# A two-layer cross-attention kernel: its beginning written out in order on every engine, with text keys by k tile and the first slot's stacks ahead of the second entry's queries

## The chip, the cores and the metric

One core of a Trainium2 chip runs the kernel. The metric is the device time of one execution in microseconds; the time before is the median of three runs. The engines are TensorE (PE, with its weight loads as PEld), VectorE (DVE), ScalarE (ACT), GpSimd (POOL) and SyncE (SP), whose queue issues nearly all transfers.

## The reference

Two cross-attention layers in turn, each on 16 entries of 256 tokens x 320 channels with a context of 256 x 512 per entry, 20 heads of 16. The first 77 context rows are text in layer 0, the others image tokens (in layer 1 all but the last four are text). Cut to what matters, layer 0 is:

```python
q = x @ Wq; k_text = text @ Wk; v_text = text @ Wv
ip_k = ip @ Wk_ip; ip_v = ip @ Wv_ip
text_out = softmax(q_h k_h^T * scale) v_h
text_probs = softmax(q k_text^T * scale)          # all heads together
sem = (text_probs @ text) @ ip^T * scale
ip_out = (softmax(q_h ip_k_h^T * scale + 0.5 * sem) * spatial_mask) ip_v_h
x = (text_out + ip_out) @ Wout + bout + x
```

Layer 1 is alike, with the semantic term by head and normalised. All is float32; the kernel splits operands into a rounded part and a rest ("halves", `hi` and `lo`) and adds three products for one.

## The kernel before

The work of a layer is cut into 80 slots: 16 entries times 5 groups of 4 heads. For a slot k of layer 0 the tiles `ks` and `qs` (a ring of four pairs, the "stack") hold up to 127 rows: keys or queries in three parts (48 rows, loaded back from DRAM, `kd` and `qd`, where they were written in another layout), 77 rows of the semantic term (`M` in `ks`, the text probabilities `tph` in `qs`), and two rows for the maxima (fields `ind0` through `mt` in `ks`, the maxima through `mt` in `qs`). `stacks0(k, parts)` issues these loads: K, Q, T (`tph`) and M. `score0` makes the scores (PE, bank S) and their maxima (DVE), `maxima0` turns the maxima and sends them into `qs`, `turned0` makes the turned scores (bank T), whose exponentials go on to `attend0` (values).

Ahead of the slots of an entry stand its tasks, generators that are advanced a step at a time: `k0` (keys, for a pair of entries), `q0` (queries), `m0t` (`tokens0`, the gram of text and image rows, tile `M`), `s0` (`semantic0`: products, softmax, transposes, `tph`, and the factor `rs`) and `v0` (three value parts). For the first pair, `keys_first` makes the keys; the text keys are made one column block m after the other, each over all four k tiles of 128 context channels.

What sets the order: everything behind `begin()` is scheduled with PE alone pinned to the written order, other engines follow the scheduler's own estimate. `begin()` (L1165) is pinned on all engines. But the loads and splits of the first weights, contexts and x (`all_halves`, L220, called at L286 to L304), the constants (zeroing of `ks`, `qs`, `vr`; L309 to L335) and the load of the fields (`ind0`, L311) stand ahead of `begin()`, outside the pinned part, so the scheduler places them among its instructions. All loads go through one helper (`dma`, L83) on SP's queue. A load of the second and third dozen waits for the landing of the one eight places earlier, since eight semaphores serve them in turn.

PSUM banks: three X, two T, one P, and S. Before, every product of the tasks goes to X.

Of the kernel before, what the change touches and what calls it, by code (L numbers as in the profile page):

```python
# [49 lines left out]
def xattn2(  # L50
# [38 lines left out]

    def bank(tag="X"):  # L90
        return ps.tile([128, 512], F32, tag=tag, name=tag, bufs=BANKS[tag])
# [35 lines left out]
    nc.scalar.copy(ident_r, ident)  # L127
    tmask = const_tile([128, 7], "tmask")
    dma(tmask, tmask_d)
# [90 lines left out]
    def all_halves(jobs, rings):  # L220

        waiting = []
        for src, hi, lo, tag in jobs:
            while sum(w[3] == tag for w in waiting) == rings[tag]:
                halves(*waiting.pop(0)[:3])
            raw = buf(tag, [128, 512], bufs=rings[tag])
            raw = raw[:, : src.shape[1]] if len(src.shape) == 2 else raw.rearrange("p (k n) -> p k n", k=src.shape[1])
            dma(raw, src)
            waiting.append((hi, lo, raw, tag))
        for w in waiting:  # L230
            halves(*w[:3])

# [29 lines left out]
    def context(b, n, wait=0):  # L262
# [9 lines left out]
        if n == 2:  # L272
# [3 lines left out]

    ct = [buf(t, [128, 2, 512], FR, bufs=2, name="ct") for t in ("cta", "cta", "ctb", "ctb")]
    ctx0 = [(cT_d[k * 128 : (k + 1) * 128, : 2 * S], ct[k][:, 0], ct[k][:, 1]) for k in range(4)]
# [6 lines left out]
    RINGS = {"P": SIZES["NP"], "raw": SIZES["RAW"], "rawc": 2}  # L285
    all_halves(  # L286
        [job for k in range(4) for job in (
            (*ctx0[k], ("rawc", "raw")[k // 2]), (rows(wk0_d, k), *rounded(wkt[:, k]), "P"))],
        RINGS,
    )  # L290
    x0 = buf("xq", [128, 3, S])
    dma(x0, xT_d[0].rearrange("(k p) t -> p k t", p=128))
    all_halves(
        [(rows(wq0_d, k), *rounded(wqt[:, k]), ("rawc", "raw")[k // 2]) for k in range(3)]
        + [(rows(wki0_d, k), *rounded(w), "P") for k, w in enumerate(wkit)],
        RINGS,
    )
    nc.vector.tensor_scalar_mul(wqt[:, 2, CH : 2 * CH], f(wqt[:, 2, CH : 2 * CH]), tmask[:, 3:4])
    wvt, wvit = buf("wC", [128, 2, 4, 320], FR), [buf("wD", [128, 2, 2, 320], FR, bufs=2) for j in range(2)]
    all_halves(  # L300
        [(rows(wv0_d, k), wvt[:, 0, k], wvt[:, 1, k], ("rawc", "raw")[k % 2]) for k in range(4)]
        + [(rows(wvi0_d, k), wvit[k // 2][:, 0, k % 2], wvit[k // 2][:, 1, k % 2], ("rawc", "raw")[k % 2]) for k in range(4)],
        RINGS,
    )  # L304
    wv0, wvi0 = [lambda s, k: wvt[:, s, k]], [lambda s, k: wvit[k // 2][:, s, k % 2]]
    wq, wo = [lambda s, k, m: wqt[:, k, columns(s, m)]], []

# [3 lines left out]
    ind0 = buf("raw", [128, 512], bufs=SIZES["RAW"], name="ind0")[:2, :S]  # L311
    dma(ind0, ind0_d)
    ind0r = buf("mt", [8, S], FR, name="ind0r")[:2]
    nc.scalar.copy(ind0r, ind0)
    for i in range(SIZES["NR"]):
        nc.gpsimd.memset(f(ks[i]), 0.0)
        nc.gpsimd.memset(f(qs[i]), 0.0)
        dma(ks[i][XROW + T0 : KS0], ind0r.unsqueeze(1).to_broadcast([2, 4, S]))
# [3 lines left out]
    for v in vr:  # L322
        nc.gpsimd.memset(v, 0.0)
        for t in range(2):
            nc.vector.tensor_scalar_add(
                vcols(v, V0W)[:, t, :, 16], vcols(v, V0W)[:, t, :, 16], tmask[:, t : t + 1]
            )
        nc.vector.memset(vcols(v, V0W)[:, 2, :, 16], 1.0)
# [3 lines left out]
    nc.vector.memset(zone, 0.0)  # L332
    nc.vector.memset(zone[:, 21:22], 1.0)
    hsn = const_tile([128, 3, 8, 2, 16], "hsn")
    nc.gpsimd.memset(f(buf("q", [128, 2, 3, S], FR))[64:, :, 2], 0.0)  # L335
# [37 lines left out]
    def keys_first():  # L373
# [6 lines left out]
        for w, lo, hi, a, z in ((wk0, 0, T0 + 1, 0, T0), (wki0, T0 - 1, S, T0, S)):  # L380
            for m in range(3):
                kp = bank()[:, : 2 * (hi - lo)].rearrange("p (b t) -> p b t", b=2)
                prod_m(kp, w, m, lambda s, k: ct(s, k)[:, :, lo:hi], 4)
                n = 64 if m == 2 else 128
                evacuate(kst[m][:, 0, :, a:z], kst[m][:, 1, :, a:z], kp[:, :, a - lo : z - lo], m)
                if a:
                    keys_out(kd[0][0], m, kst[m], slice(0, 1))
                else:
                    nc.gpsimd.tensor_copy(kt[:n, m, :, :, :T0], f(kst[m][:n, :, :, :T0]))
                yield  # L390
# [188 lines left out]
    def split(src, neg, eng, tag):  # L579

        hl = buf(tag, [128, 5, S], FR)
        order = queued if tag == "hq" else lambda inst: inst
        order(nc.scalar.copy(hl[:, 0:3], src))  # L583
        order(eng.tensor_sub(hl[:, 3:5], src[:, 0:2], f(hl[:, 0:2])))  # L584
        order(nc.vector.scalar_tensor_tensor(hl[:, 2], f(hl[:, 2]), neg, src[:, 2], op0=ALU.mult, op1=ALU.add))  # L585
        return hl

# [42 lines left out]
    def queries0(b):  # L630
        x = x0 if b == 0 else load(xT_d[b], "xq")
        yield
        xs = split(x, tmask[:, 5:6], nc.gpsimd if b else nc.vector, "hq")
        yield
        return (yield from queries(0, xs))
# [529 lines left out]
    def begin():  # L1165
        parts = lambda *keys: [step(key) for key in keys if key in tasks]
        k0, q0, s0, m0, q1 = ("k0", 0), ("q0", 0), ("s0", 0), ("m0t", 0), ("q0", 1)
        parts(k0, k0, k0, q0, q0, q1, q0, q0, q0)
        get(*q0)
        get(*m0)  # L1170
        parts(s0, s0, s0, s0, s0)
        stacks0(0, "M")
        stacks0(1, "M")
# [121 lines left out]
```

## Time and profile before

| | us |
|---|---|
| median of three runs (1550.27 to 1552.6) | 1551.0 |
| the profiled execution | 1552.99 |
| its span, first to last instruction | 1551.2 |
| granted PE clock over the span | 0.971 |
| PE busy | 1450.1 |
| DVE busy | 1220.5 |
| POOL busy | 1193.5 |
| ACT busy | 872.6 |

A row of a timeline gives the start from the beginning of the span, the duration, the engine, the line of the kernel, the operation, `out<-in` with the tiles' names, the shape and how many equal instructions follow each other; in brackets the time that the engine was idle ahead of it and what ended that. SPq and ACTq are the engines' queues issuing transfers. A row of a stretch gives the busy time and count of PE, PEld, DVE, ACT and POOL, then PE's granted clock (1 is full), the DMA engines' busy share and GB/s.

### The profile page before, as it was taken

What the parts mean: (1) busy time and instruction counts of PE and PEld (TensorE: products, weight loads), DVE (VectorE), ACT (ScalarE), POOL (GpSimd) and SP (SyncE); (2) the same over time, 40 slices, a digit from 0 to 9 for tenths busy, and PEclk for the clock granted to TensorE, in tenths of its full rate; (3) what the DMA queues carried; (4) which work ended last, traced back from release to release, by engine and by line L of the source; (5) the groups of instructions that cost most, each with busy time, mean ns of one, the idle gap of its engine ahead of it and who ended that gap; (6) DMA issues with size and microseconds to landing.
All of it is one profiled execution on the core that took longest, in us unless ns stands there. A gap on an engine that the chain in (4) does not pass through costs nothing.

```text
span 1551.2 us, 36088 instructions
## 1 busy us (share of the span) xinstructions
PE 1450.1 (93%) x12726; PEld 1170.3 (75%) x12726; DVE 1220.5 (79%) x2687; ACT 872.6 (56%) x1941; POOL 1193.5 (77%) x1246
## 2 busy tenths in 40 slices
PE   6789999999999989878999999999999999999996
PEld 6668787888787878656777777777777777777764
DVE  6468877778887788878778887888888888788785
ACT  5335464556464545536566666666656665666561
POOL 4248797889797877768578798878887898779785
PEclk9889999999999999889999999999999999999998
DMA  6755767676767665666344344434444444433411
GB/s 210 196 180 153 220 189 213 181 219 189 218 191 214 180 206 165 189 181 178 102 137 124 109 123 129 124 110 142 110 114 124 126 116 118 137 106 99 118 32 36
DMA packets 228815, 233.04 MB, mean 150 GB/s; under 512 B 38410, under 2 KB 198508, under 8 KB 228620
## 3 DMA queue, kind: packets, MB, share of 16 engines
q1 hardware_dynamic: 226428, 229.44, 51.6%
q8 instruction: 102, 1.67, 0.5%
q10 hardware_dynamic: 2208, 1.30, 0.3%
q14 instruction: 77, 0.63, 0.1%
HBM read 118.04 MB, written 77.10 MB: 126 GB/s over the span
## 4 chain that ended last, share of the span: by engine, by line
PE 33%; POOL 7%; DVE 6%; ACT 2%; issue 2%; DMA 1%; ACTq 1%; SPq 0%; DVEq 0%; POOLq 0%
PE X L923 11%; PE X L238 5%; POOL wt L914 5%; PE P L935 3%; PE X L595 3%; PE P L945 3%; PE T L875 2%; PE S L881 2%; DVE wt L924 2%; PE X L1048 1%; POOL hq L584 1%; DVE ho L585 1%; DVE mn L883 1%; ACTq L905 1%; PE X L248 1%
## 5 line engine op out<-in xcount | busy, mean ns | idle before, releaser
L758 POOL TENSOR_TENSOR P<-P,rs 128x512 f32<-128x512 f32 x320 | 412.8, 1311 | 126.9 <-ACT P L755 126.7
L914 POOL TENSOR_TENSOR wt<-P,ctb 128x512 f32<-128x512 f32 x320 | 410.3, 1307 | 88.7 <-ACT ctb L913 87.8
L923 PE MATMUL X<-ctb,gm 128*128 128x512 f32 x1120 | 306.5, 403 | 6.4 <-DVE wt L924 6.3
L755 ACT ACTIVATE P<-T 128x512 f32<-128x512 f32 x320 | 176.1, 594 | 177.0 <-PE T L752 107.1
L924 DVE TENSOR_TENSOR wt<-X,wt 128x512 f32<-128x512 f32 x320 | 216.7, 682 | 47.0 <-PE X L923 40.8
L923 PEld LDWEIGHTS X<-ctb,gm 128*128 128x128 f32 x1120 | 196.2, 189 | 39.6 <-DVE wt L924 9.2
L895 ACT ACTIVATE P<-T 128x512 f32<-128x512 f32 x320 | 173.3, 594 | 79.3 <-PE T L875 76.0
L913 ACT ACTIVATE ctb<-P 128x512 fp32r<-128x512 f32 x320 | 187.4, 627 | 47.8 <-PE X L923 35.9
L883 DVE TENSOR_REDUCE mn<-S 128x4 fp32r<-128x1008 f32 x160 | 191.3, 1195 | 0.0
L730 DVE TENSOR_REDUCE mn<-S 128x4 fp32r<-128x716 f32 x160 | 142.3, 889 | 0.0
L785 PE MATMUL P<-P,vr 128*32 128x256 f32 x1920 | 129.9, 404 | 2.8 <-DVE mx L665 1.8
L728 PE MATMUL S<-ks,qs 125*128 125x256 f32 x640 | 119.5, 311 | 9.0 <-DMA qs<-tph 4.8
L728 PEld LDWEIGHTS S<-ks,qs 125*128 125x128 f32 x640 | 90.7, 199 | 45.0 <-issue 36.6
L752 PE MATMUL T<-qs,ks 127*128 127x256 f32 x640 | 110.4, 294 | 13.8 <-DVE tmp L802 7.7
L1011 POOL TENSOR_TENSOR r<-u,rs 128x40 f32<-128x40 f32 (+2 forms) x17 | 108.7, 6394 | 3.8 <-DVE u L1008 3.8
L752 PEld LDWEIGHTS T<-qs,ks 127*128 127x128 f32 x640 | 92.8, 198 | 17.1 <-DVE tmp L802 8.1
L729 DVE TENSOR_REDUCE mn<-S 128x4 fp32r<-128x308 f32 x160 | 74.2, 463 | 30.1 <-PE S L728 29.5
L796 DVE STREAM_TRANSPOSE nt<-P 128x512 f32<-128x512 f32 x80 | 56.9, 711 | 47.7 <-PE P L785 47.2
L785 PEld LDWEIGHTS P<-P,vr 128*32 128x32 f32 x1920 | 58.3, 115 | 45.8 <-issue 9.4
L595 PE MATMUL X<-hq,wE 128*128 128x256 f32 x512 | 80.4, 297 | 9.0 <-ACT hq L583 4.3
L935 PE MATMUL P<-P,v1t 128*32 128x256 f32 x1280 | 86.5, 388 | 0.2 <-DVE wt L924 0.2
L945 PE MATMUL P<-wt,zone 128*32 128x256 f32 x1280 | 85.1, 379 | 0.3 <-DVE wt L924 0.3
(231 smaller groups left out, 3011.9 us busy)
## 6 DMA issues: line engine op xcount, KB each, us to landing
qd<-q SPq DMA_DIRECT2D x96, 256.0 KB
qs<-tph SPq DMA_DIRECT2D x64, 308.0 KB
rawc<-in_cT_dram SPq DMA_DIRECT2D x60, 256.0 KB
qs<-qd SPq DMA_DIRECT2D x80, 192.0 KB
ks<-kd SPq DMA_DIRECT2D x80, 192.0 KB
ks<-kd SPq DMA_DIRECT2D x160, 96.0 KB
qs<-qd SPq DMA_DIRECT2D x160, 96.0 KB
kd<-kst SPq DMA_DIRECT2D x57, 256.0 KB
```

Of the source, the lines that this page charges most:

```text
L728: mm(sp[:, h], Q[: XROW + T0, h, t * 128 : (t + 1) * 128], K[: XROW + T0, h], start=True, stop=True)
L730: anchor(nc.vector.tensor_reduce(mn[:, t, :, 1], sp[:, :, T0:], axis=AX.X, op=ALU.max))
L752: mm(st[p][:, j], K[:KS0, 2 * p + j, t * 128 : (t + 1) * 128], Q[:KS0, 2 * p + j], start=True, stop=True)
L755: exp = anchor(nc.scalar.activation(pt, st[p], AF.Exp, scale=SCALE))
L758: anchor(nc.gpsimd.tensor_mul(pt, pt, rs[:, t : t + 1].to_broadcast([128, 2, S])))
L785: mm(pv[32 * s : 32 * s + 32, o : o + S], v[:, vt, h : h + 32], P[k, s // 2][:, t, s % 2], start=vt < 2, stop=vt != 1,)
L883: anchor(nc.vector.tensor_reduce(maxes[k + 2][:, t], sp[:, :, :T1], axis=AX.X, op=ALU.max))
L895: anchor(nc.scalar.activation(P[k, u][:, t], st[u], AF.Exp, scale=SCALE))
L913: nc.scalar.activation(R[k, u][:, t], P[k, u][:, t], AF.Copy, scale=0.5)
L914: anchor(nc.gpsimd.tensor_sub(W[k, u][:, t], P[k, u][:, t], f(R[k, u][:, t])))
L923: mm(yp, gm[:, gb], R[k, u][:, kt], start=i == 0, stop=i == len(blocks[n]) - 1)
L924: nc.vector.tensor_mul(W[k, u][:, n], yp, W[k, u][:, n])
```

## The change

The loads, splits, constants and fields move from ahead of `begin()` into it, as the functions `land`, `cast`, `constants`, `marks` and `fields`, so that their place is written on all engines. x is the ninth load. The text keys run with the k tile outermost, in three banks at once, each tile's products right behind its split. `turns` lends the banks T and P to some products of the beginning in place of X. The gram of entry 1 moves ahead of the semantic products of entry 0; the image keys' weights are split between the pieces of `s0`. The queries of entry 1 move behind the first loads of slot 0's stack, which are issued in the order T, Q, K (and so for slot 1). The zeroing of `qs` is left out, that of `vr` is cut to the columns that nothing else writes, and the marks in `vr` move from DVE to POOL.

```diff
@@ (bank)
+    turns = []
+
     def bank(tag="X"):
+        tag = turns.pop(0) if turns and tag == "X" else tag
         return ps.tile([128, 512], F32, tag=tag, name=tag, bufs=BANKS[tag])
...
+    def fields():
+
+        ind0 = buf("nt", [128, 2, 8, 32], bufs=2, name="ind0").rearrange("p a f c -> p (a f c)")[:2, :S]
+        dma(ind0, ind0_d)
+        ind0r = buf("mt", [8, S], FR, name="ind0r")[:2]
+        nc.scalar.copy(ind0r, ind0)
+        for i in range(SIZES["NR"]):
+            dma(ks[i][XROW + T0 : KS0], ind0r.unsqueeze(1).to_broadcast([2, 4, S]))
...
@@ (keys_first)
-        for w, lo, hi, a, z in ((wk0, 0, T0 + 1, 0, T0), (wki0, T0 - 1, S, T0, S)):
...
+        kp = [out(0, T0 + 1) for m in range(3)]
+        for k in range(4):
             for m in range(3):
...
+                terms = ((0, 0), (0, 1), (1, 0))[: 3 if m < 2 else 2]
+                for i, (a, c) in enumerate(terms):
+                    mm(kp[m], wk0(a, k, m), ct(c, k)[:, :, : T0 + 1], start=k + i == 0, stop=k == 3 and i == len(terms) - 1)
+            yield
...
@@ (begin, before)
-        parts(k0, k0, k0, q0, q0, q1, q0, q0, q0)
         get(*q0)
         get(*m0)
-        parts(s0, s0, s0, s0, s0)
-        stacks0(0, "M")
-        stacks0(1, "M")
-        parts(k0, k0, k0, s0, q1, q1, q1, q1)
-        stacks0(0, "QK")
-        get(*s0)
-        stacks0(0, "T")
-        stacks0(1, "QKT")
-        get("v0", 0)
...
@@ (begin, after)
+        for k in range(4):
+            land(("c", k), ("k", k))
+        dma(x0, xT_d[0].rearrange("(k p) t -> p k t", p=128))
+        dma(tmask, tmask_d)
+        constants()
+        for k in range(4):
+            turns.extend(["X"] * (3 if k == 0 else 0))
+            cast(("c", k), ("k", k))
+            parts(k0)
+            if k < 3:
+                land(("q", k))
+        nc.scalar.copy(ident_r, ident)
+        land(*named("i"))
+        xs0.append(split(x0, tmask[:, 5:6], nc.vector, "hq"))
+        for k in range(3):
+            cast(("q", k))
...
+        land(("v", 0), ("v", 1), ("v", 2))
+        fields()
+        marks()
+        turns.extend(["T", "T", "P", "X", "X", "X", "T"])
+        get(*m0)
+        parts(k0)
+        parts(q0, q0, q0, q0)
+        stacks0(0, "M")
+        parts(q0)
+        get(*q0)
+        cast(("i", 0), ("i", 1))
+        get(*m1)
+        parts(s0)
+        cast(("i", 2))
+        parts(s0)
+        cast(("i", 3))
+        parts(s0, s0, s0)
+        stacks0(1, "M")
+        parts(q1)
+        turns.extend(["X", "T", "X", "X"])
+        parts(k0)
+        parts(s0)
+        cast(("v", 0), ("v", 1), ("v", 2))
+        land(("v", 3), *named("w"))
+        parts(k0)
+        cast(("v", 3))
+        parts(k0)
+        stacks0(0, "T")
+        stacks0(0, "QK")
+        parts(q1)
+        cast(*named("w"))
+        get(*s0)
+        parts(v0, q1, q1)
+        stacks0(1, "TQK")
+        parts(v0)
+        score0(0, 0)
+        parts(q1)
...
```

Three places as they stand in the built programs. First ACT in the middle of the beginning, before: the cast of the fields (`mt<-ind`) stands late, between the first and second part of q.

```order
L583 CAST hq_303<-xq_129 128x768
L150 CAST wC_168<-rawc_90 128x320
L150 CAST wC_168<-raw 128x320
L150 CAST wD<-raw 128x320
L150 CAST wD<-rawc_89 128x320
L150 CAST wD<-rawc_90 128x320
L150 CAST q_244<-X 128x256
L150 CAST wD<-raw 128x320
L314 CAST mt_209<-ind_207 2x256
L150 CAST q_244<-X 128x256
```

ACT now, from the cast of x on (`nt` is the buffer that holds the fields):

```order
L269 CAST hq_215<-xq_87 128x768
L151 CAST wE_82<-rawc_110 128x320
L151 CAST wE_82<-rawc_111 128x320
L151 CAST wE_82<-raw 128x320
L327 CAST mt_239<-nt_236 2x256
L418 ACTIVATE M_251<-T 77x179
L151 CAST kst_148<-X 128x2x77
L151 CAST kst_149<-X 128x2x77
L245 CAST ho_150<-X 64x2x77
L246 COPY both_275<-X 64x154
L151 CAST q_134<-T 128x256
L151 CAST q_134<-P 128x256
```

The cast of the fields now stands ahead of the gram (`M`), of all text keys (`kst`, `ho`) and of q.

Second PE between the transposes of the text probabilities and the values of entry 0 (`wC`), before:

```order
L670 MATMUL X<-ident,sp_371 77x128
L670 MATMUL X<-ident,sp_372 77x128
L595 MATMUL X<-hq_303,wE_84 128x256 x16
L598 MATMUL X<-hq_303,wE_84 128x256 x5
L679 MATMUL X<-tph_450,M_346 128x256
L680 MATMUL X<-tph_450,M_346 128x256
```

PE now, from the last product of `rs` to behind the first score (S):

```order
L673 MATMUL X<-tph_407,M_251 128x256
L226 MATMUL X<-wC_88,cta_77 128x320 x3
L226 MATMUL X<-wC_88,cta_78 128x320 x3
L226 MATMUL X<-wC_88,ctb_79 128x320 x3
L226 MATMUL X<-wC_88,ctb_80 128x320 x3
L588 MATMUL X<-hq_215,wE_82 128x256 x16
L226 MATMUL X<-wD,cta_77 128x320 x3
L226 MATMUL X<-wD,cta_78 128x320 x3
L226 MATMUL X<-wD,ctb_79 128x320 x3
L226 MATMUL X<-wD,ctb_80 128x320 x3
L721 MATMUL S<-ks_95,qs_91 128x256 x4
L591 MATMUL X<-hq_215,wE_82 128x256 x5
```

The queries of entry 1 (`hq`) have moved behind the product of `rs` and the first value part, their third part (x5) behind the first score.

Third SP's queue from the last half of entry 0's keys (`kd<-ho`) on, before:

```order
L83 DMA kd_66<-ho_252 64x256
L83 DMA xq_129<-in_xT_dram 128x3x256
L83 DMA qd_457<-q_244 128x2x256 x3
L83 DMA qd_457<-q_244 64x2x256
L83 DMA qd_457<-q_244 64x256
L83 DMA qs_199<-qd_308 48x1024
L83 DMA ks_203<-kd_66 48x4x256
L83 DMA qs_199<-tph_450 77x4x256
L83 DMA qs_200<-qd_308 48x1024
L83 DMA ks_204<-kd_66 48x4x256
L83 DMA qs_200<-tph_450 77x4x256
```

SP now, from the same row on (behind it follow the six writes of entry 1's keys, `kd`, and the stack of slot 2):

```order
L83 DMA kd_66<-ho_150 64x256
L83 DMA qs_91<-tph_407 77x4x256
L83 DMA qs_91<-qd_282 48x1024
L83 DMA ks_95<-kd_66 48x4x256
L83 DMA qs_92<-tph_407 77x4x256
L83 DMA qs_92<-qd_282 48x1024
L83 DMA ks_96<-kd_66 48x4x256
L83 DMA qd_493<-q_134 128x2x256 x3
L83 DMA xq_87<-in_xT_dram 128x3x256
L83 DMA qd_493<-q_134 64x2x256
L83 DMA qd_493<-q_134 64x256
```

The stacks of slots 0 and 1 have moved ahead of entry 1's queries (`qd<-q`); before, the stack of slot 2 stood ahead of the writes of entry 1's keys, now behind them.

More of the change, by code (lines that the diff above doesn't have):

```diff
@@ L284, in xattn2 @@
     wki0 = lambda s, k, m: wkit[k][:, columns(s, m)]
[L285 to L290, printed above, removed]
-    x0 = buf("xq", [128, 3, S])
[L292 to L297, printed above, removed]
@@ L309, in xattn2 @@
     qs = [const_tile([128, 4, S], f"qs{i}", FR) for i in range(SIZES["NR"])]
     ks = [const_tile([128, 4, S], f"ks{i}", FR) for i in range(SIZES["NR"])]
[L311 to L318, printed above, removed]
@@ L577, in tokens1 @@
         return V, G
[L579 to L586, printed above, removed]
     def project(l, w, a, evac):
@@ L630, in queries0 @@
     def queries0(b):
-        x = x0 if b == 0 else load(xT_d[b], "xq")
+        x = b and load(xT_d[b], "xq")
         yield
-        xs = split(x, tmask[:, 5:6], nc.gpsimd if b else nc.vector, "hq")
+        xs = split(x, tmask[:, 5:6], nc.gpsimd, "hq") if b else xs0.pop()
         yield
```

106 lines of the change are left out of this document (58 added, 48 removed).

## The prediction, made before the result was known

> **What bounds the kernel now.** I read the busy shares and the slices of the page first (one row each), then stretches of 50 us (busy us of PE, its weight loads, DVE, ACT and POOL, then PE's granted clock, DMA share and GB/s), then the first 65 us engine by engine.
>
> ```profile
> PE 1450.1 (93%) x12726; PEld 1170.3 (75%) x12726; DVE 1220.5 (79%) x2687; ACT 872.6 (56%) x1941; POOL 1193.5 (77%) x1246
> ...
> PE   6789999999999989878999999999999999999996
> ```
>
> ```profile
> 0.00:50.00 50.00, 32.80 (x172) 30.45 (x172) 25.66 (x88) 23.32 (x56) 17.01 (x27) 0.96 0.69 213
> 50.00:100.00 50.00, 42.23 (x288) 37.69 (x289) 29.61 (x58) 19.67 (x48) 19.57 (x18) 0.80 0.60 175
> ...
> 150.00:200.00 50.00, 47.23 (x441) 40.88 (x441) 42.40 (x98) 26.29 (x65) 40.51 (x41) 1.00 0.72 216
> ```
>
> TensorE (PE) bounds it: 93% of the span, nines in most slices. The first slices are the exception. From 0 to 50 us PE is busy 32.80 of 50, from 150 to 200 it is 47.23. The change rewrites just this beginning. The chain that ended last can be followed back only to 735 us, so it says nothing of the beginning; the argument has to be that PE's order behind the beginning is row for row the same, and that PE is nearly full there: what the first slots gain, the end gains. I take the first product of slot 0's turned scores (L752 before), which opens the steady loop, as the mark. PE's timeline leads to it (start, us, line, tiles, count, and in brackets the idle time ahead and what ended it):
>
> ```profile
> 30.20 1.14 PE L238 MATMUL X<-ctb,wB 128*128 128x360 f32 x6
> ...
> 36.13 3.30 PE L595 MATMUL X<-hq,wE 128*128 128x256 f32 x15 [0.96 <-POOL hq L584]
> ...
> 40.22 0.28 PE L680 MATMUL X<-tph,M 77*128 77x256 f32 x1
> 44.75 1.04 PE L238 MATMUL X<-wD,ctb 128*128 128x320 f32 x6
> 50.56 1.19 PE L728 MATMUL S<-ks,qs 125*128 125x256 f32 x4 [4.77 <-DMA qs<-tph]
> 51.55 1.80 PE L238 MATMUL X<-wC,cta 128*128 128x320 f32 x6
> 64.26 0.71 PE L728 MATMUL S<-ks,qs 125*128 125x256 f32 x4
> 64.81 0.64 PE L752 MATMUL T<-qs,ks 127*128 127x256 f32 x4
> ```
>
> The mark stands at 64.81. The first score (L728) starts at 50.56, after 4.77 us of empty PE, when the stack of slot 0 lands; slot 2's first score, which PE has just ahead of the mark, at 64.26. Two things delay the first score: entry 1's queries (36.13, in front of `rs`, which ends at 40.50), and the stack's three loads, issued behind all of that.
>
> **The change, part by part.** Durations are those of the rows; each time is what I work out for the changed kernel.
>
> *Text keys by k tile.* First and last casts of this part on ACT, the last on DVE, PE's last products:
>
> ```profile
> 4.03 0.62 ACT L150 CAST cta<-rawc 128x512 fp32r<-128x512 f32 x1 [2.01 <-DMA rawc<-in_cT_dram]
> ...
> 9.44 0.46 ACT L150 CAST wA<-P 128x320 fp32r<-128x320 f32 x1
> ```
>
> ```profile
> 10.20 0.63 DVE L153 TENSOR_TENSOR wA<-P,wA 128x260 fp32r<-128x260 f32 x3
> ```
>
> ```profile
> 14.39 1.06 PE L248 MATMUL X<-ctb,wA 128*128 128x156 f32 x4
> ```
>
> Now the last products end at 15.45. The last weight tile is ready at 10.83; with k outermost only its 8 products follow, 8 x 0.26 (1.06 for 4) = 2.1 us: 12.9. The work is unchanged.
>
> *x early, queries of entry 0.* PE's queries, grams and semantic products of entry 0, then ACT's cast of x and of the small field `ind0`:
>
> ```profile
> 19.50 3.57 PE L595 MATMUL X<-hq,wE 128*128 128x256 f32 x15 [1.12 <-DVE hq L584]
> 22.87 1.27 PE L598 MATMUL X<-hq,wE 128*128 128x256 f32 x5
> 23.93 1.16 PE L238 MATMUL X<-cta 128*77 128x192 f32 x6
> ...
> 25.62 1.73 PE L651 MATMUL X<-kb,q 128*128 128x156 f32 x12
> ```
>
> ```profile
> 16.91 0.83 ACT L583 CAST hq<-xq 128x768 fp32r<-128x768 f32 x1
> ...
> 24.07 0.40 ACT L314 CAST mt<-ind 2x256 fp32r<-2x256 f32 x1
> ```
>
> x was the seventeenth load and is now the ninth. The eight loads ahead are four of 128 x 512 and four of 128 x 384 floats, 256 and 192 KB; between the casts at 4.03 and 9.44 1536 KB landed in 5.4 us, 284 KB/us. So x (384 KB) is there at 10.8, is cast and split (0.83 and about as much on DVE) by 12.5, and the three query weights (192 KB each, the mask `hop` of 192 KB among them) by 13.5. PE does the grams of entry 0 (12 x 0.19 = 2.3 us) to 15.2, then 16 query products (0.24 each, 3.8) to 19.0, not 23.07. **A new wait** stands here: ACT's row `mt<-nt` needs `ind0`, a tiny load now queued behind the four image weights and three value weights (4 x 192 + 3 x 160 KB, 4.4 us: landing at 18), and behind that row ACT holds every evacuation: gram, three keys, q. It ends at 18.4, and PE's next product (q's third part) needs the first key bank, free at about 19.3. So it costs PE 0.3 us as I have it; every us that `ind0` is later costs one. Third part 1.3, grams of entry 1 (new at this place) 2.3, semantic products 1.7: done at 24.7, before 27.35. The zeroing of `qs` that falls away, and marks on POOL in place of DVE, count nothing: POOL has long gaps here.
>
> *Image keys and `rs`.* Entry 1's queries leave this stretch. What stays is 32 products of image keys (1.14 for 6, overlapping to 0.16 each: 5.2 us), transposes and `rs` (0.9). DVE must split the four image weights (0.6 each) in between, against softmax pieces; I let that cost 0.8. `rs` ends at 31.5, not 40.50: 9 us earlier.
>
> *Stack of slot 0.* The last half of the keys on DVE, and SP's first load of the stack:
>
> ```profile
> 34.20 0.52 DVE L260 TENSOR_TENSOR ho<-X,both 64x358 fp32r<-64x358 f32 x1
> ```
>
> ```profile
> 43.18 0.57 SPq L83 DMA_DIRECT2D qs<-qd  x1
> ```
>
> Keys finished at 34.72 before, about 32.5 now (PE at 30.6, then two copies and two subtractions). The loads follow at once, in the order tph, q, k. From the first issue to the first score it was 50.56 - 43.18 = 7.4 us; now the last load waits besides for the keys to be written, which I put at 1 us: first score at 41. PE has meanwhile one value product and entry 1's queries (1.8 + 3.3 + 1.8), which fit in. Gain so far 9.5 us.
>
> *From the first score to the mark.* Here most of the gain is spent again. SP has now, behind the first score, entry 1's queries, x of entry 2, the second half of the keys, and only then slot 2's stack, whose score PE has in front of the mark, and slot 0's maxima. The sizes of these transfers, and four stretches of 10 us:
>
> ```profile
> qd<-q SPq DMA_DIRECT2D x6, 256.0 KB
> qs<-tph SPq DMA_DIRECT2D x4, 308.0 KB
> xq<-in_xT_dram SPq DMA_DIRECT2D x3, 384.0 KB
> kd<-kst SPq DMA_DIRECT2D x4, 256.0 KB
> ks<-kd SPq DMA_DIRECT2D x5, 192.0 KB
> ks<-M SPq DMA_DIRECT2D x4, 215.4 KB
> ```
>
> ```profile
> 0.00:10.00 10.00, 3.38 (x10) 2.56 (x10) 4.17 (x15) 5.48 (x11) 9.43 (x16) 1.00 0.74 240
> ...
> 40.00:50.00 10.00, 5.79 (x41) 5.53 (x39) 1.19 (x3) 2.83 (x6) 0.23 (x1) 0.96 0.82 226
> 50.00:60.00 10.00, 9.34 (x53) 9.15 (x54) 2.92 (x5) 1.74 (x4) 0.00 (x0) 0.70 0.67 209
> ...
> 70.00:80.00 10.00, 7.19 (x42) 5.77 (x45) 7.59 (x9) 5.22 (x11) 6.59 (x6) 0.67 0.69 174
> ```
>
> Slot 1's stack is 308 + 192 + 192 = 692 KB (q rows are as many as k rows); q 3 x 256 and, for its third part, 192 in proportion to rows and copies = 960; x 384; the keys likewise 960; slot 2's stack 192 + 192 + 308 + 215 = 907. Together 3903 KB or 4.0 MB. At 220 GB/s, between the two stretches in which the queue was full of this kind, that takes 18 us: slot 2's score at 59, the mark at 59.6. **The mark comes 5.2 us earlier** (64.81 - 59.6). PE alone would be there sooner: q's third part 1.3, three value parts of entry 1 and one of entry 0 at 1.8 each, scores and semantic products some 4, together 12.5 with full clock. At 240 GB/s, the pace of the first 10 us, the mark is at 58.2; at 174, the lowest of these stretches, at 64.6, no gain. I take 220, since the same transfers ran at 226 and 209.
>
> *Behind the mark.* Loads of the next context pair follow slot 1's maxima on SP in both kernels, so they move along. Elsewhere the scheduler's order of ACT, DVE, POOL and SP changes in some rows where layer 0 gives way to layer 1. That stretch, and the longest wait on a transfer in the chain near it:
>
> ```profile
> 660.00:680.00 20.00, 12.61 (x101) 9.15 (x101) 15.48 (x31) 6.36 (x13) 12.62 (x11) 0.83 0.46 125
> ```
>
> ```profile
> 734.96 4.07 DMA qs<-mt
> ```
>
> PE has holes there, and one wait on a transfer is worth up to 4.1 us. The rows swap places with neighbours, so I take 0 and bound it by 4 on both sides.
>
> **Sum.** The profiled execution took 1552.99 with a span of 1551.2, 2.0 above the median of 1551.0. Its span becomes 1551.2 - 5.2 = 1546.0, and the median 1545.8.
>
> **A clock that the trace shows.** The six value products at 51.55 took 1.80, the same at 44.75 1.04: behind the empty 4.77 us PE ran at about half speed, and the granted clock of 50 to 60 us is 0.70. [...]
>
> **Rivals.**
> 1. *The clock stays up.* The row at 50.56 has the only gap over 3 us; with the new order I find none that long up to the mark, and the stretch of 50 to 100 us has a clock of 0.80. If the beginning kept 0.95 instead, PE's 42.23 us would shrink by about 6, and not all of it is on the path: a total of 5.2 + 4 to 6, about 1541. Against it: other half-speed stretches (70 to 80 us, 0.67) follow gaps that the change leaves.
> 2. *The queue takes it all.* At 174 GB/s, or with 5 us more of SP waits for q and keys, slot 2's stack lands where it did: 1551 less a few tenths to 2, about 1550. For it: SP now stands in the middle of this queue waiting for q's third part, which comes only behind the first score. Against: 226 and 209 above.
> 3. *Slower: the mark passes its old place.* The same single queue: slot 0's maxima, 4 issues, stand behind 4.0 MB, where before (row below) they found SP idle. If the transfers interleave so that less than 150 GB/s comes out, slot 2's stack lands after 67.7 and the mark after 68.3: 3.5 us late, 1554.5. Below about 172 it decides against the change. Nothing shows such a rate with the queue full; 1 in 7.
>
> ```profile
> 57.84 2.58 SPq L740 DMA_DIRECT2D qs<-mt  x4
> ```
>
> **How the numbers follow.** Forecast (mark 3.5 to 8 us earlier) 0.48 at 1545.8, own range 1543 to 1547.7; clock 0.20 at 1541; queue 0.18 at 1550; slower 0.14 at 1554.5. About 0.2% (3.1 us) is what a measurement of this kernel can tell. Faster: 0.46 of the forecast's, all of the clock's and a little of the queue's, 0.67; same 0.18; slower 0.15. The range from 1538 to 1552 leaves out most of the slower case and some of the clock's best, under 0.2.
>
> **What would show it.** Text keys ending near 13 us; ACT's `mt<-nt` at 18, with the four key and gram evacuations right behind; `rs` ending near 31.5; the first score at 41, waiting for `ks<-kd`; slot 2's score waiting for a DMA of its stack near 59 and the mark right behind; from there the same distances as before. I am wrong if the first score is early but the mark is not (rival 2), if ACT waits past 20 for `ind0`, or if the mark is early and the end is not: then the layer change has eaten it.

## The result, and the profile after

The changed kernel takes 1552.1 us in the median of 12 executions (1546.9 to 1561.9); the kernel before, on the same chip, 1552.2 (1549.7 to 1555.9). The ratio is 1.0008 with an interval of 0.9991 to 1.0026: no difference. The forecast was 1545.8, the range ended at 1552. The profiled execution of the changed kernel is its slowest, 1561.86 with a span of 1560.1, some 10 us above its median, so its trace shows where time can go, and not how much goes there each time.

The page of the changed kernel, busy share and slices of PE, then the clock that PE was granted in the same slices:

```profile
PE 1459.4 (94%) x12726; PEld 1174.0 (75%) x12726; DVE 1219.5 (78%) x2678; ACT 872.4 (56%) x1941; POOL 1188.9 (76%) x1251
...
PE   7789999999999899878999999999999999999996
...
PEclk9799999999999998889999999999999999999998
```

Its beginning, in PE's timeline; the last two rows are the score of slot 2 and the mark:

```profile
8.96 3.94 PE L380 MATMUL X<-ctb,wA 128*128 128x156 f32 x16
...
17.73 0.75 PE L591 MATMUL X<-hq,wE 128*128 128x256 f32 x5
...
20.42 0.83 PE L644 MATMUL T<-kb,q 128*128 128x156 f32 x6
...
28.69 0.28 PE L673 MATMUL X<-tph,M 77*128 77x256 f32 x1
...
32.50 1.09 PE L226 MATMUL X<-wC,ctb 128*128 128x320 f32 x3 [2.21 <-ACT wC L151]
...
36.32 3.57 PE L588 MATMUL X<-hq,wE 128*128 128x256 f32 x15 [1.07 <-POOL hq L270]
...
42.12 0.64 PE L721 MATMUL S<-ks,qs 125*128 125x256 f32 x4
...
56.79 0.71 PE L721 MATMUL S<-ks,qs 125*128 125x256 f32 x4 [0.99 <-DMA ks<-M]
57.33 0.64 PE L745 MATMUL T<-qs,ks 127*128 127x256 f32 x4
```

The mark stands at 57.33, before at 64.81: 7.5 us early, more than the 5.2 that were forecast. The lead lasts for a while: the 18th group of scores is 8.3 us early (129.11 against 137.40). Then it goes. To see where, I cut both executions at the same groups of scores, which are numbered in the order of PE, the first as 0: from the mark (group 3) to group 120, to group 168, to the last (318). The rows are stretches, with columns as before.

Before:

```profile
64.26:541.50 477.24, 448.93 (x4098) 383.43 (x4097) 371.22 (x824) 256.09 (x597) 385.02 (x368) 0.97 0.68 196
541.50:754.16 212.66, 183.36 (x1603) 148.63 (x1601) 170.29 (x377) 106.95 (x248) 153.91 (x161) 0.92 0.63 181
754.16:1500.54 746.38, 736.15 (x6532) 570.43 (x6529) 617.80 (x1322) 468.20 (x1005) 602.77 (x650) 1.00 0.41 115
```

After:

```profile
56.79:540.07 483.28, 452.32 (x4098) 385.22 (x4098) 365.33 (x821) 256.78 (x597) 386.11 (x368) 0.96 0.68 195
540.07:763.27 223.20, 191.77 (x1603) 153.78 (x1601) 177.44 (x377) 107.25 (x248) 153.78 (x161) 0.87 0.61 172
763.27:1509.58 746.31, 736.48 (x6531) 569.99 (x6529) 616.81 (x1322) 468.14 (x1005) 603.30 (x650) 1.00 0.41 115
```

The same products take 6.0 us longer in the steady slots (483.28 against 477.24), 10.5 longer around the change of layer (223.20 against 212.66), and exactly as long in layer 1. PE's count is the same; what differs around the change of layer is its clock, 0.87 against 0.92, and PE is *busier* (191.77 against 183.36) with the same products. One place shows how. PE's timeline of the changed kernel from 589 us, and its clock in three adjoining windows:

```profile
589.37 0.41 PE L226 MATMUL X<-kst,wB 128*128 128x64 f32 x2 [1.38 <-ACT wB L151]
590.16 0.30 PE L226 MATMUL X<-kst,wB 128*128 128x64 f32 x1 [0.39 <-DVE wB L154]
...
594.08 2.60 PE L226 MATMUL X<-kst,wB 128*128 128x64 f32 x12
596.61 2.79 PE L778 MATMUL P<-P,vr 128*32 128x256 f32 x24
```

```profile
587.28:590.70 3.42, 1.66 (x14) 1.43 (x14) 3.28 (x7) 1.89 (x6) 2.14 (x2) 1.00 0.79 218
590.70:600.94 10.24, 9.93 (x56) 7.55 (x55) 6.62 (x22) 2.74 (x10) 3.73 (x5) 0.50 0.35 97
600.94:604.35 3.41, 3.41 (x28) 3.41 (x27) 1.73 (x6) 2.03 (x5) 2.59 (x3) 1.00 0.31 88
```

And the same rows before:

```profile
591.42 0.30 PE L238 MATMUL X<-kst,wB 128*128 128x64 f32 x1 [0.31 <-DVE wB L153]
...
593.78 1.42 PE L238 MATMUL X<-kst,wB 128*128 128x64 f32 x12
595.13 1.50 PE L785 MATMUL P<-P,vr 128*32 128x256 f32 x24
```

A wait of 1.8 us left PE busy for 1.66 of 3.42 us; for the next 10.24 us it ran at half speed, and 24 products that took 1.50 took 2.79. A wait of under 2 us cost 5 more behind it (half of the 9.93 us that PE was busy in that stretch). In each of the two traces PE's clock changes on one grid of 3.41 us, and behind the mark half-speed stretches are 3.41, 6.83 or 10.24 us long. From the mark to the end of layer 0 they add up to 64.9 us before and 99.0 after.

So the theory of the prediction ("then the layer change has eaten it", by the order of ACT, DVE, POOL and SP there) had rivals: that the half-speed windows fall by luck, or that something else made the waits.

### The profile page after: what moved, and what is told of

The parts are those of the page before. It is cut to its first block, busy times and chain, and to the rows that moved or that the text cites. A ratio compares the mean times of both kernels' runs of the same rounds, so it can differ in the third digit from the quotient of the medians.

```text
span 1560.1 us, 36074 instructions
## 1 busy us (share of the span) xinstructions
PE 1459.4 (94%) x12726; PEld 1174.0 (75%) x12726; DVE 1219.5 (78%) x2678; ACT 872.4 (56%) x1941; POOL 1188.9 (76%) x1251
## 4 chain that ended last, share of the span: by engine, by line
PE 63%; DVE 10%; POOL 8%; DMA 8%; issue 4%; ACT 4%; SPq 2%; ACTq 1%; DVEq 0%; POOLq 0%
PE X L226 13%; PE X L916 11%; PE P L778 6%; PE X L588 6%; POOL wt L907 5%; PE S L721 4%; PE T L745 4%; PE P L928 4%; PE P L938 3%; PE T L868 2%; PE S L874 2%; DMA qs<-qd 2%; SPq L83 2%; PE X L236 2%; PE X L591 2%
## 5 line engine op out<-in xcount | busy, mean ns | idle before, releaser
L917 DVE TENSOR_TENSOR wt<-X,wt 128x512 f32<-128x512 f32 x320 | 216.7, 682 | 48.5 <-PE X L916 42.1
L778 PE MATMUL P<-P,vr 128*32 128x256 f32 x1920 | 134.5, 414 | 3.0 <-POOL P L751 1.6
L778 PEld LDWEIGHTS P<-P,vr 128*32 128x32 f32 x1920 | 58.5, 116 | 48.7 <-issue 12.9
L938 PE MATMUL P<-wt,zone 128*32 128x256 f32 x1280 | 85.1, 379 | 0.3 <-DVE wt L917 0.3
L588 PE MATMUL X<-hq,wE 128*128 128x256 f32 x496 | 76.9, 294 | 5.2 <-POOL hq L270 2.9
```

Source lines behind the costliest of these rows:

```text
L778: mm(pv[32 * s : 32 * s + 32, o : o + S], v[:, vt, h : h + 32], P[k, s // 2][:, t, s % 2], start=vt < 2, stop=vt != 1,)
L917: nc.vector.tensor_mul(W[k, u][:, n], yp, W[k, u][:, n])
```

## Experiments

Group numbers are those of the scores, as above. "Held" means that every row of ACT, DVE, POOL and SP behind the beginning is chained to its forerunner, so that the scheduler has no choice left:

```diff
+    for engine, order in ORDER.items():
+        traced = [i for i in nc.cur_bb.bb.instructions if i.engine == getattr(mybir.EngineType, engine) ...][::-1]
+        for a, b in zip(order, order[1:]):
+            tc.add_manual_dep(traced[b], traced[a].name, ...NoSync..., reason="order")
```

**The changed kernel again.** No edit.

> The changed kernel once more, unchanged. Two theories of where the beginning's gain went. Layer change (as the prediction put it): the new order of ACT, DVE, POOL and SP rows where layer 0 gives way to layer 1 costs it each time; then the profile shows the lead over before at 8 us up to 540 us and the whole loss of 8 to 10 us between 560 and 745 us, and the times lie close together. Clock: the half-speed windows behind the beginning (3.41 or 6.83 us long, on a grid of 3.41 us) fall on other holes from one execution to the next; then the first turned score is again at 57.3 +- 0.5 and the lead at 110 us again 8, but the lead is lost at other places than 160, 390, 475 and 590 to 720 us, the times scatter over 10 us or more (1547 to 1562), and they follow the mean granted clock by about 1.5 us per 0.001.

1553.7 (1546.1 to 1560.6, 12 executions), before in the same session 1552.6; ratio 1.0012 (0.9985 to 1.0039). The mark is at 57.3 again. In this execution, of 1556.3, the two stretches were:

```profile
56.72:541.02 484.30, 451.76 (x4097) 384.75 (x4097) 369.41 (x821) 256.38 (x597) 385.85 (x368) 0.96 0.68 195
541.02:759.40 218.38, 183.34 (x1603) 147.98 (x1601) 177.78 (x377) 107.10 (x247) 153.72 (x160) 0.92 0.61 173
```

Half-speed time to the end of layer 0 is 78.5 us, and part of it lies elsewhere: groups 40 to 60 took 85.1 us where the first execution had 78.0, groups 20 to 40 took 77.1 and not 80.3. So the windows do move from one execution to the next. But both executions lose 6 to 7 us in the steady slots, ahead of the layer change, against the one of before; this speaks against the layer change theory, and made me doubt that it was luck alone.

**Beginnings and orders exchanged.** `old_change` is the changed kernel held in the order of rows of before, `old_begin` the kernel before held in the order of the changed kernel.

> The changed kernel's beginning with every row of ACT, DVE, POOL and SP behind the beginning in the order that the kernel before has. Layer change theory: the loss behind 560 us is gone, 1544 +- 2, 8 us under before. Clock theory: the order is not it, the median stays within 2 us of the changed kernel's own and the scatter stays as wide (10 us or more).

> The kernel before with its own beginning, and every row of ACT, DVE, POOL and SP behind it in the order of the changed kernel. Layer change theory: it bears the loss without the gain, 1560 +- 2, 8 us over before. Clock theory: within 2 us of before (1552); how wide it scatters tells whether the scatter belongs to the order behind or to the beginning.

`old_change` takes 1540.5 (ratio 0.9938, 0.9915 to 0.9961), `old_begin` 1552.1 (0.9999, 0.9966 to 1.0031). The first, some 3.5 us below what the layer change theory expected, still looks like it; the second contradicts it: the new order under the old beginning costs nothing. Holding may itself do something, so both need controls.

**Held in their own order.**

> The changed kernel with every row of ACT, DVE, POOL and SP behind the beginning held in the very order that it has; only what the scheduler may still choose differs (which PSUM bank a product writes). A control for the two exchanged kernels. If the order at the layer change is what costs the gain, it stays at 1552 +- 2, 12 us over the changed beginning with the old order (1540.5). If the placement of banks that came with it is what costs, it falls to 1540 to 1544, near the other held kernels with the new beginning (1540.5, and 1546.8 with entry 1's queries first). If only the clock scatters, it stays at 1552 with a spread of 14 us.

> The kernel before with every row of ACT, DVE, POOL and SP behind the beginning held in the very order that it has; the other control. If the order at the layer change is what costs, it stays at 1552 +- 2. If the bank placement costs, it falls too, and stands over the changed beginning with the same order (1540.5) by what the beginning brings, 7 to 9 us: 1548 to 1550.

| rows held in the order of | beginning of before | changed beginning |
|---|---|---|
| before | 1549.1 | 1540.5 |
| the changed kernel | 1552.1 | 1542.0 |
| not held | 1551.4 to 1553.7 | 1552.1, 1553.7 |

(`held_after`: ratio 0.9930, 0.9900 to 0.9959; `held_before`: 0.9980, 0.9952 to 1.0008.) Down the columns the order is worth 1.5 to 3.0 us, which medians of 12 executions that spread over 13 to 23 us do not tell from nothing: the layer change theory has fallen. Across the rows the beginning is worth 8.6 and 10.1 us, with the same scatter on them; at the mark it is only 4.2 and 5.6 (57.47 against 61.70, and 56.67 against 62.30). So the 7.5 us of the two free kernels at the mark hold about 2 to 3 us that before's rows need not cost: before's profiled execution ran at half speed from 49.2 to 56.0 us, and with the same rows held PE ran at full speed there:

```profile
49.76 0.71 PE L728 MATMUL S<-ks,qs 125*128 125x256 f32 x4 [3.06 <-DMA qs<-tph]
```

And holding a kernel in *its own order* gains 10 to 12 us for the changed one (for before some 2, within the interval). What a held kernel does not share with a free one, with the same rows, is the place of its results, which the scheduler chooses by its own estimate of when a place comes free: above all the PSUM bank of each product. The built programs tell: of 2136 PSUM tiles 529 lie in another bank in `held_after` than in the changed kernel. (Among the other tiles only `wt`, in layer 1, takes its buffers in another turn, and layer 1 takes 746.3 and 745.0 us.) Between the two held orders with the new beginning it is 46, and between two held kernels of one order, with the old and the new beginning, none behind the beginning: across the rows of the table the banks are alike. And between before and the changed kernel 165 differ behind the beginning, in groups at each pair of entries and around the layer change. I had compared rows, in which a bank has no number.

The waits fit. PE at the maxima behind group 42, before and after:

```profile
237.22 0.23 PE L736 MATMUL X<-ident_r,mn 128*8 128x128 f32 x1 [0.55 <-DVE mn L730]
```

```profile
232.44 0.28 PE L729 MATMUL X<-ident_r,mn 128*8 128x128 f32 x2 [1.25 <-ACT P L748]
```

Before, this product waits for its own operand. After, it waits for ACT's exponentials: in the changed kernel's program it lies in the bank of the turned scores ahead of it, which ACT has still to read; in before's and in the held one it lies in a bank of keys that was read long ago.

**The table of banks, by itself.** Three twins: the changed kernel, its rows held in its own order, all PSUM as one tile, and each product's place from a table. The table of `held_placed` is the changed kernel's, that of `held_replaced` is the one of `held_after`; `placed_2` and `replaced_2` repeat them; `placed_before` has before's banks in everything behind the beginning.

```diff
+    PLACES = ("...",)   # a digit for each product: its bank
+    psum = ps.tile([128, 4096], F32, tag="psum", name="psum", bufs=1)
...
-        return ps.tile([128, 512], F32, tag=tag, name=tag, bufs=BANKS[tag])
+        at = 512 * int(PLACES[len(placed)])
+        placed.append(tag)
+        return psum[:, at : at + 512]
```

> The changed kernel with its rows held in its own order, and every product's PSUM bank written in from a table: the very banks that the scheduler chose for the changed kernel. Bank theory (the scheduler's choice of banks, made anew when the beginning moved its estimate, puts maxima and turned scores into banks whose readers are not done): the loss is back, 1552 +- 3, with the waits of the maxima for ACT's exponentials at the scores 42 and 82 and of the turned scores for DVE behind score 147. Rival (the held order itself brought the 10 us, whatever the banks): 1542 +- 3.

> The same kernel and the same way of placing, but with the table of banks that the scheduler chose for the kernel whose rows were held (1542). Bank theory: 1542 +- 3, 10 us under its twin. Rival: as its twin. Should both stand at 1552, the way of placing costs and the pair says nothing of the table's worth.

> The twin with the table of banks of the changed kernel (held_placed) once more. Bank theory: 1546 to 1548, 5 to 6 us over its twin. Rival (the first difference was scatter): within 2.5 us of its twin. With both looks the waits behind the scores 121, 140 and 147 should again be those of the changed kernel (2.4 to 2.8, 1.8 to 2.5 and 5.3 us).

> The twin with the other table (held_replaced) once more. Bank theory: 1540 to 1542; none of the three waits of its twin. Rival: 1543 to 1545, as its twin.

> The twin once more (changed beginning, its rows held, banks from a table), now with the banks that the scheduler chose for the kernel before in all products behind the beginning. Bank theory in its narrow form (what the change lost, it lost since the scheduler chose other banks than before): 1542 to 1544, without the maxima's waits of 1.7 us for ACT behind score 42, but with those of 2.4, 1.8 and 5.3 us behind the scores 121, 140 and 147, which before has too. Rival (the banks that cost are those that both kernels have): 1546 to 1548, as with the changed kernel's own table.

| table of | median | ratio to before, interval |
|---|---|---|
| the changed kernel | 1546.5; 1547.1 | 0.9968 (0.9950 to 0.9985); 0.9952 (0.9927 to 0.9977) |
| `held_after` | 1540.6; 1544.0 | 0.9942 (0.9921 to 0.9963); 0.9930 (0.9903 to 0.9957) |
| before | 1538.4 | 0.9906 (0.9872 to 0.9940) |

The sizes missed what was expected. `held_placed` lies between the bank theory (1552) and its rival (1542), 3 us either way; `replaced_2` missed 1540 to 1542 and fell where its rival had it; `placed_before` lies below its 1542 to 1544. The order of the tables is the bank theory's each time: within a session the changed kernel's table is 5.9 and 3.1 us slower than that of `held_after`, though the intervals of these pairs overlap. All executions together, 24 with the changed kernel's table have a median of 1546.8, 12 with the other 1540.9, 7 with before's, in a later session, 1538.4; the interval of these 7 is clear of that of `held_placed` and touches that of `placed_2`. With the same rows on every engine, the changed kernel's banks cost 3 to 6 us against those of `held_after` and some 8 against before's. PE's rows at the maxima behind group 42 with the changed kernel's table, then with before's:

```profile
225.83 0.29 PE L756 MATMUL psum<-ident_r,mn 128*8 128x128 f32 x2 [1.73 <-ACT P L775]
```

```profile
225.93 0.23 PE L756 MATMUL psum<-ident_r,mn 128*8 128x128 f32 x1 [0.40 <-DVE mn L750]
```

This wait for ACT stands behind group 42 in all four executions with a trace that have the changed kernel's banks (1.25, 2.41, 1.73 and 1.66 us) and in none of the others, where it is 0.9 us or less and not for ACT. A half-speed stretch of 6.83 us follows in two of the four (of 3.41 us in before and in `replaced_2`, behind the shorter wait).

And with before's table the place at which the profiled execution lost 5 us, with the 24 products at full speed again:

```profile
579.79 0.28 PE L253 MATMUL psum<-kst,wB 128*128 128x64 f32 x1
...
581.89 1.42 PE L253 MATMUL psum<-kst,wB 128*128 128x64 f32 x12
583.25 1.50 PE L805 MATMUL psum<-P,vr 128*32 128x256 f32 x24
```

Groups 131 to 133 took 10.2 us here and 10.5 in before; with the changed kernel's banks 15.2, 14.5, 15.3 and 15.4 in all four executions with a trace (with the table of `held_after` 11.5 to 14.8). The longest wait is one that both kernels have: behind group 147 a turned score lies in the bank of the values that DVE still settles. With the changed kernel's table and with that of `held_after`:

```profile
653.85 0.80 PE L772 MATMUL psum<-qs,ks 127*128 127x256 f32 x2 [5.28 <-DVE tmp L822]
```

```profile
657.35 2.79 PE L805 MATMUL psum<-P,vr 128*32 128x256 f32 x24 [2.74 <-DVE tmp L822]
```

With before's table it is 5.28 us as well, and yet that table is no slower than the one of `held_after`: the length of one wait is not its price.

**Own banks for each kind.**

```diff
+        ring = {"T": (3, 4), "P": (2,), "X": (5, 6, 7)}[tag]
+        at = 512 * ring[placed.count(tag) % len(ring)]
```

> The same held rows, but each kind of product in banks of its own, in strict turn: X in three, T in two, P in one, S in its pair. No product can then meet a bank that another kind still reads. Bank theory in its simple form (only foreign readers cost): 1536 to 1542. Rival: a strict turn of three X banks makes PE wait for evacuations that a free choice avoids, 1546 or more.

1639.3 (ratio 1.0568, 1.0545 to 1.0591), as its rival had it: the simple form of the bank theory, that only foreign readers cost, is wrong by far. Most of it lies in layer 1, which all other kernels here run in 745 to 749 us, and there in products that wait for their bank's last reader (the three costliest follow the stretch: us in total, times, the longest):

```profile
777.48:1582.36 804.88, 749.96 (x6529) 561.89 (x6528) 622.50 (x1321) 467.37 (x1005) 600.93 (x652) 1.00 0.38 107
```

```profile
PE psum L598 <- DVE kst L255: 16.8, 14, 1.2
PE psum L583 <- DVE wt L924: 16.0, 14, 1.3
PE psum L923 <- DVE wt L924: 10.4, 16, 0.8
```

**One part of the beginning undone.** In `q1_first`, held in the changed kernel's order, the queries of entry 1 stand in front of the stacks again.

```diff
+        get(*q1)
         stacks0(0, "T")
         stacks0(0, "QK")
-        parts(q1)
```

> The changed kernel with one part undone: the queries of entry 1 stand again in front of slot 0's stack and rs; every row behind the beginning is held in the changed kernel's order. Both theories: the first score and the mark (first turned score) come later by the 21 query products, 3.3 + 1.8 us, less what hid in the wait for the stack: mark at 60 to 62 in place of 57.3. Layer change theory: the end moves with the mark, 3 to 5 us over the changed kernel. Clock theory: the end moves by 3 to 5 us only on the mean, in a scatter of 10.

1546.8 (0.9970, 0.9945 to 0.9995), 4.8 us over `held_after`, which behind the beginning has the same banks and differs in this alone (the two ran in different sessions, and their intervals overlap). The mark comes later than expected, at 65.5 and not at 60 to 62, since the first score waits for its stack again:

```profile
38.48 0.79 PE L591 MATMUL X<-hq,wE 128*128 128x256 f32 x5
...
49.53 1.19 PE L721 MATMUL S<-ks,qs 125*128 125x256 f32 x4 [5.98 <-DMA ks<-kd]
...
65.53 0.64 PE L745 MATMUL T<-qs,ks 127*128 127x256 f32 x4
```

This part alone makes the lead at the mark; the end shows 5 of its 8 us. But the mark of `q1_first` is later than that of every kernel with the old beginning (61.7 to 64.8), and its median lies below all of theirs (1549.1 to 1553.7): the mark alone does not foretell the end.

**The windows filled.** Products of the unit matrix that nobody reads, in front of the maxima and the first turned scores of some slots, into banks that the next product writes anyway: 27 slots on top of `held_replaced` (`fill`), nine on top of `old_change` (`fill_few`, in which 29 of the 2136 tiles changed their banks besides).

```diff
+    holes = (10, 20, 30, 40, 50, 60, 69, 72, 74)
...
+        if k - 1 in holes:
+            for i in range(4):
+                mm(mp[:, 256:], ident_r, wide, start=True, stop=True)
```

> The kernel of the second table (held_replaced) with products of the unit matrix that nobody reads put in front of the maxima and of the first turned scores of 27 slots (10, 20, 30, 40, 50 and 58 to 79), four each, about 0.14 us apiece: 30 us of PE work, into banks that the next product writes anyway. Clock theory (short waits cost 3.4 us or more since they switch to half speed): half-speed time from the mark to the end of layer 0 falls from about 55 us to 30 or less and the time by 5 to 10 us, to about 1535. Rival (the half-speed windows are cheap, or the added products delay the real ones): 1545 to 1555.

> The changed beginning with the old order held (old_change, 1540.5) and unread products of the unit matrix in nine slots alone (10, 20, 30, 40, 50, 60, 69, 72, 74), where each held kernel had empty PE time in front of the maxima or the turned scores: 72 products of 0.14 us, 10 us, nearly all in that empty time. Clock theory: no half-speed window in the steady slots, half speed from the mark to the end of layer 0 at 45 us or less, 1535 to 1538 and a spread under 8 us. Rival (what the added products cost is what the windows cost, as with 27 slots): 1540 to 1542.

`fill` takes 1541.0 (0.9936, 0.9917 to 0.9954), no less than its twin, and so neither the 1535 of the clock theory nor the 1545 of its rival. Its half-speed time fell to 37.5 us from 68.3 and 51.2 in its twin's two traces, and its 6 executions lie within 4.8 us of each other, the 6 of its twin in the same session within 6.5; but around the layer change PE carries 195.2 us of work in place of 185.3, which costs what the windows cost. `fill_few` takes 1535.1 (0.9866, 0.9845 to 0.9887; 1532.5 to 1537.3), 5.4 us under `old_change` and 18.7 under before: the fastest kernel here. Its 5 executions and the 12 of `old_change` come from two sessions, and the 29 moved tiles were not tried without the products. From group 20 to group 120, first `held_after`, then `fill_few`:

```profile
139.89:530.18 390.29, 375.39 (x3505) 321.85 (x3501) 307.81 (x700) 214.70 (x500) 329.40 (x316) 0.99 0.69 201
```

```profile
137.08:524.13 387.05, 374.89 (x3544) 323.55 (x3540) 307.69 (x700) 214.83 (x500) 329.42 (x316) 1.00 0.71 204
```

In the changed kernel this stretch took 399.2 and 400.2. With the products added PE is no busier than without: it stays at full speed from group 20 to 120. Part of this is luck: the twins with the changed kernel's table, without any such products, took 387.0 and 394.2 for the stretch.

## Why the prediction was right and wrong

- **Text keys**: right. They end at 12.90 (forecast 12.9).
- **x, queries, the wait for `ind0`**: the order of events was right, the sizes were not. ACT's cast of the fields waited 3.19 us for the landing, as forecast, but ended its wait at 16.1 and not at 18, and PE's third part of q did not feel it:

```profile
16.14 0.41 ACT L327 CAST mt<-nt 2x256 fp32r<-2x256 f32 x1 [3.19 <-DMA nt<-in_ind_dram]
```

  The semantic products end at 21.3, 3.4 us before the forecast of 24.7. I had taken the durations of q's third part and of the grams ahead of them from rows of before that stood at half speed: 5 products took 1.27 there and 0.75 here, 6 of a gram 1.16 and 0.70. PE comes to full speed at 17.26, before at 25.32.
- **`rs`**: ends at 28.97, forecast 31.5, before 40.50, mostly for the same reason.
- **First score**: 42.1, forecast 41, but not by the transfer named, so the near hit is luck. PE arrives late: 2.21 us for the values' weights and twice 1.1 for the split of x, then 15 queries at half speed (3.57), all of which I had put down as "fit in". The keys are late too. ACT waited 4.31 us for the last value weight, which the change loads behind entry 1's x and the first keys; the copy of the keys' last half, which PE had finished at 28.50, and the cast of entry 1's x stand behind that row (4.33 and 4.07 in the traces of `again` and `held_after`), a wait on ACT that the prediction does not have:

```profile
31.99 0.46 ACT L151 CAST wC<-raw 128x320 fp32r<-128x320 f32 x1 [4.31 <-DMA raw<-in_wv_dram]
32.35 0.45 ACT L245 CAST ho<-X 64x358 fp32r<-64x358 f32 x1
```

  Keys were finished at 34.4 and not at 32.5; that PE was 3.4 us ahead of the forecast until then made up for it.
- **From the first score to the mark**: right in kind. The single queue decides, slot 2's score waits 0.99 us for `ks<-M`; it moved 230 GB/s where I took 220:

```profile
42.00:57.00 15.00, 11.96 (x89) 11.40 (x89) 6.57 (x14) 4.02 (x10) 0.00 (x0) 1.00 0.78 230
```

  The mark is 7.5 us early, not 5.2; but against before's rows held it is 4.2 to 5.6. Rivals 2 and 3 did not happen; rival 2's total came out close to the truth for a reason that is not its own.
- **Behind the mark**: the step that failed. I took 0 and bounded it by 4, and wrote that PE's order "is row for row the same" and so "what the first slots gain, the end gains". PE's order is the same, and the rows that swap places at the layer change are worth 1.5 to 3 us, not clear of the scatter and within my bound. But the place of the results is no part of that order. With the new beginning the scheduler chose other banks, the maxima and others met banks that were still read, and some of these waits of 1 to 2 us were followed by half speed. Where rows behind the beginning, banks and way of holding are the same, the beginning is worth 8.6 to 10.1 us, so the argument that the end gains it holds only with the banks held still. The free changed kernel and the held one, which have the same rows and other banks, are 10 to 12 us apart; in the twins the table of banks by itself accounts for 3 to 8 of that.
- **The clock as a rival** was sought in the wrong place, and by a length of gap, 3 us, that no run shows to decide: in before 3.41 us at half speed from 35.56 follow a stretch of 3.41 us in which PE was busy for 1.09 and its longest gap was 1.92. Up to 100 us it changed little (0.86 from 50 to 100 us, before 0.80, the rival said 0.95). Behind the mark it multiplied small waits: 12.8 of the 16.5 us that the profiled execution lost against before from the mark to the last score are half of the busy time that it has more at half speed (42.3 against 29.5).

What stays open: the free changed kernel (1552.1 and 1553.7) is 5 to 7 us over its twin with the same rows and the same table (1546.8). The twin is held, and its PSUM is one tile, so that which waits stand is not quite the same; which of it counts was not tried. With the table of `held_after` the one-tile form itself is not dearer or cheaper than `held_after` (1540.6 and 1544.0 against 1542.0). The twins with one PSUM tile also have some five rows in another order where the beginning ends, alike in all of them. Nor was it followed further why PE waits behind group 130: for ACT's cast of `wB` in the first execution, in `held_placed` and, with the other table, in `held_replaced` (1.38, 1.61, 1.36), in others a score mainly for DVE's maxima (1.2 to 1.3), with before's banks for neither. The cast is an operand and no bank, so that the link from the banks to the 5 us lost there is argued, not shown.

## What to carry to other kernels

Where a scheduler places results, a change of one stage changes the program behind it even if every row there stands where it stood; compare the banks as well as the rows, or hold both, before an early gain is carried to the end. A wait of one or two microseconds on the bounding engine is to be priced with the half-speed stretch behind it, where the trace shows one: here 3.4 to 10.2 us in which half of the busy time is lost. A few unread products in waits that are there in any case, with 29 tiles in other banks besides, went with 5 us less and a spread of 4.8 in place of 13.4 us; the same in 27 slots bought nothing.

## What the runs showed of the hardware

In the traces PE's clock changes on a grid of 3.41 us, whose place against the first instruction differs from one execution to the other: 0.19 us in the first one of the changed kernel, 1.43 in the one of before. A window of this grid need not be empty to be followed by half speed: PE was busy for 1.66 of the 3.42 us ahead of the 10.24 at half speed above. Behind the beginning of these two traces every window with a busy share under 0.5 was followed by one at half speed, of those between 0.5 and 0.72 some. No sharp threshold shows: in before half speed followed 2.45 busy us of 3.41 (from 236.95), in the changed kernel full speed followed 1.74 (from 532.67). That the same waits fall into one window or across two, by chance in each execution, is argued from the grid and not shown. The places are less a matter of luck than the lengths: in before, both traces of the changed kernel, `held_after` and the five of the twins a half-speed stretch begins behind each of the groups 3, 147 and 165, and lasts 3.41, 6.83 or 10.24 us. At the start of the changed kernel products without a gap from 5.18 us on ran at half speed up to 17.26, for 12.1 us (six products of a gram took 1.17 at 13.65 and 0.70 at 18.32). Behind its mark full speed was back after one half-speed window with PE busy throughout in one place (3.41 of 3.41 us, from 546.32), and after two in another (from 471.23).
